# Side work of a scan kernel in smaller pieces, and in another order

## The chip, the cores and the metric

The kernel runs on one core of a Trainium2 chip. The metric is the device time of one execution in microseconds (us). Before the change three executions took 6510.28, 6516.89 and 6527.06 us; the median is 6516.89 us. The profile shown below is of one execution of 6514.5 us.

## The reference

Two layers follow one another. Layer 0 is a selective scan over images, layer 1 a spectral (Fourier) attention layer. The change touches only layer 0, which computes, for 4 images of 48 x 48 places and 128 channels:

```python
xz = einsum('bhwc,ec->bhwe', groupnorm(x), in_proj_w)   # 128 -> 2 x 256 channels
xin, z = split(xz)
xc = silu(depthwise_conv3x3(xin) + conv_b)              # nine taps a channel
xs = [x0, x1, x0 reversed, x1 reversed]                 # row order and column order, each both ways
dts, Bs, Cs = x_proj_w[k] @ xs[k]                       # 8 + 16 + 16 rows
dt = softplus(dt_proj_w[k] @ dts + dt_proj_b)
# for each of 256 channels and 16 states, along 2304 places:
h = h * exp(dt * A) + (dt * u) * B
y = sum over states of h * C
# the four directions are summed, D * xs is added, then layer norm over 256 channels,
# times silu(z), times out_proj_w; the result is added to x
```

Layer 1 takes the result, and its code is the same in both kernels.

## The kernel before

**Tiles and loops.** An image's 2304 places are cut into five chunks of 480 places (the last has 384). The 256 channels are two halves (`f` = 0, 1) of 128 partitions. The outermost loop runs over 16 passes, numbered here from 0: pass 4 b + q is image b (0 to 3) in the q-th direction of `ORDER = (0, 2, 1, 3)`. Directions 0 and 2 go along the rows, forwards and backwards, 1 and 3 along the columns. A pass has 5 chunks, a chunk has 16 steps, one for each state, so there are 1280 steps.

**A step** is spread over the engines by `advance`, which calls ten small stages with different lags, so that ten steps are under way at a time. In a step TensorE spreads one row of B over 128 partitions (`spread`, tile `pb`, skipped in one step of four); VectorE multiplies it by dt * u (`drive_in`, tile `db`); ScalarE computes the two halves of exp(dt * A) (`decay`, tile `da`, in PSUM) and copies the carry of the last chunk; VectorE runs the recurrence along the chunk (`scan`, tile `h`); GpSimd multiplies by C (`read_out`, tile `hc`); TensorE adds the two halves to the sums over states by multiplying with the identity (`sum_up`, tile `yp`). In the one step of four that has no `pb`, GpSimd makes `db`.

**Side work.** Everything else of layer 0 is written as Python generators that wait in the queue `later`, and is interleaved with the steps. A call of `piece()` takes the next generator and lets it emit instructions up to its next `yield`. `advance` calls `piece()` once at the end of every step. A bare `yield` keeps the generator as the current one, so that the next piece is also its own. `yield FREE` lets the next piece start again at the head of the queue, and `yield WAIT` passes the turn on at once. What is emitted in a piece stands in each engine's queue right behind the step's own instructions, because `Ordered` keeps all instructions of an engine in the order in which they are written. Side tiles in PSUM all use the one bank with tag `pp` (`side`) after the start.

These are the generators:

- `boot` prepares image 0: for each chunk the input projection (`project_in`, tiles `pj` and `pad`), the convolution (`convolve`, tiles `pc` and `xc`, nine matmuls with diagonal matrices `cdiag`, one a tap), and the chunk's projections (`project_chunk`: `px`, two matmuls; two small corrections with `less`; `pd`, two matmuls). In pass 0 a second `piece()` follows every step.
- `front(b)` does the same for a whole further image b, apart from the chunk projections. Each half first has nine `taps` and a memset of `pad` on GpSimd, then five input projections, then five convolutions. It ends with a Silu over all of `xc`.
- `project` does the chunk projections of the next pass, and waits (`WAIT`) when it is a ring of seven chunks ahead.
- `back` ends a chunk of an image: after its last direction, layer norm (tiles `pm`, `pv`), the gate (`pz`), the output projection (`po`, `pr`) and the store. Its work tile `ws` has the same single buffer (tag `pad`) that `front` uses for `pad`, and both use the single buffer of `x`. So the next image's `front` can't be started before the last `back` has ended.

**Order of the side work before.** `upcoming` appends the next pass's `project` at the end of `later`. At the start of chunk 2 of an image's first pass, all remaining `back`s are drained, that is, their pieces are emitted one after the other without steps between, and then `front(b + 1)` is appended. At the start of the image's last pass, `drain(coming)` emits what is left of `front`. `drain(nxt)`, close to the end of each pass, does the same for the next pass's `project`.

**Pieces before.** `convolve` yields after every third tap, and goes on with the next chunk's first taps in the piece in which it emits the copy of the previous one; `front` yields `FREE` only around whole halves. `project_chunk` has both `px` matmuls in one piece. `back` yields twice after `pm`, after `po` and after `pr`.

Of the kernel before, what the change touches and what calls it, by code (L numbers as in the profile page):

```python
# [19 lines left out]
B, T, H, W = 4, 48, 48, 128  # L20
# [33 lines left out]
def layer0(ctx, tc, io, x1_dram):  # L54
# [107 lines left out]
    def like(ap, k):  # L162

        return ap if k % 2 == 0 else ap.rearrange("p (w h) -> p w h", h=T)
# [32 lines left out]
    def project_in(b, f, x, made, pad, s, n):  # L197

        r0, nr = s // H, n // H
        pj = side(f"pj{b}_{f}_{s}")  # L200
        on.tensor.matmul(
            pj[:, 0:n], made["w"][:, f * 128 : (f + 1) * 128], x[:, 0, s : s + n], start=True, stop=True
        )
        yield
        on.scalar.activation(
            pad[:, 1 + r0 : 1 + r0 + nr, 1 : 1 + H],
            pj[:, 0:n].rearrange("p (r c) -> p r c", c=H),
            AF.Identity,
            bias=made["wb"][:, f : f + 1],
        )  # L210

    def convolve(b, f, cdiag, pad, xc, s, n):
        r0, nr = s // H, n // H
        pc = side(f"pc{b}_{f}_{s}")
        for j in range(9):
            dy, dx = divmod(j, 3)
            on.tensor.matmul(
                pc[:, 0:n].rearrange("p (r c) -> p r c", c=H),
                cdiag[:, j],
                pad[:, r0 + dy : r0 + dy + nr, dx : dx + H],  # L220
                start=(j == 0),
                stop=(j == 8),
            )
            if j % 3 == 2:
                yield
        on.scalar.activation(xc[:, f, s : s + n], pc[:, 0:n], AF.Identity, bias=cb[:, f : f + 1])

# [29 lines left out]
    def front(b, made):  # L257


        x = load_x(b, "x")  # L260
        yield FREE
        yield from open_up(b, x, made)
        xc = made["xc"]
        for f in range(NF):
            cdiag = one.tile([128, 9, 128], F32, tag="cdiag", name=f"cdiag{b}_{f}")
            taps(cdiag, f)
            pad = one.tile([128, T + 2, H + 2], F32, tag="pad", name=f"pad{b}_{f}")
            on.gpsimd.memset(pad, 0.0)
            yield FREE
            for s, n in CHUNKS:  # L270
                yield from project_in(b, f, x, made, pad, s, n)
            for s, n in CHUNKS:
                yield from convolve(b, f, cdiag, pad, xc, s, n)
            yield FREE
        for f in range(NF):
            on.scalar.activation(xc[:, f], xc[:, f], AF.Silu)
        yield
# [6 lines left out]
    def project_chunk(c, w_dt, xc):  # L284


        k, s, n = c.k, c.s, c.n
        src = at(xc, k, s, n)
        px = side(f"px{c.t}")
        for f in range(NF):  # L290
            on.tensor.matmul(
                like(px[0:NX, 0:n], k), w_xp[:, k, f], src[:, f], start=(f == 0), stop=(f == NF - 1)
            )
        yield
        xd = two.tile([32 + R, LC], F32, tag="xd", name=f"xd{c.t}")
        on.scalar.copy(xd[:, 0:n], px[0 : 32 + R, 0:n])
        c.cd = dram.tile([2 * N, LC], F32, tag="cd", name=f"cd{c.t}")
        nc.sync.dma_start(c.cd[:, 0:n], xd[0 : 2 * N, 0:n])

        c.bs = ring.tile([NX, LC], BF16, tag="bs", name=f"bs{c.t}")  # L300
        on.scalar.copy(c.bs[:, 0:n], px[0:NX, 0:n])
        for q in range(2):
            on.tensor.matmul(px[0:NX, 0:n], less[:, q], c.bs[:, 0:n], start=False, stop=True, skip_group_check=True)
            yield
            rows = slice(64 + 32 * q, NX)
            on.scalar.copy(c.bs[rows, 0:n], px[rows, 0:n])
        c.dt = ring.tile([128, NF, LC], F32, tag="dt", name=f"dt{c.t}")
        for f in range(NF):
            pd = side(f"pd{c.t}_{f}")
            on.tensor.matmul(  # L310
                pd[:, 0:n],
                w_dt[32 : 32 + R, f * 128 : (f + 1) * 128],
                xd[32 : 32 + R, 0:n],
                start=True,
                stop=True,
            )
            yield
            on.scalar.activation(c.dt[:, f, 0:n], pd[:, 0:n], AF.Identity, bias=b_dt[:, k, f : f + 1])
# [22 lines left out]
    def back(b, s, n, yb, x, w, wb):  # L341


        t = f"{b}_{s}"
        xs = at(x, 1, s, n)[:, 0]
        ys = yb[:, :, 0:n]
        ws = one.tile([128, (T + 2) * (H + 2)], F32, tag="pad", name=f"ws{t}")
        z = ws[:, 0 : NF * LC].rearrange("p (f n) -> p f n", f=NF)
        rs, xo = ws[:, NF * LC : (NF + 1) * LC], ws[:, (NF + 1) * LC : (NF + 2) * LC]
        pm = side(f"pm{t}")  # L350
        for f in range(NF):
            on.tensor.matmul(pm[:, 0:n], lnmat, yb[:, f, 0:n], start=(f == 0), stop=(f == NF - 1))
        yield
        yield
        on.vector.tensor_sub(ys, ys, pm[:, None, 0:n].to_broadcast([128, NF, n]))
        yield
        on.scalar.activation(z[:, :, 0:n], ys, AF.Square)
        pv = side(f"pv{t}")
        for f in range(NF):
            on.tensor.matmul(pv[:, 0:n], lnmat, z[:, f, 0:n], start=(f == 0), stop=(f == NF - 1))  # L360
        yield
        on.scalar.activation(rs[:, 0:n], pv[:, 0:n], AF.Sqrt, bias=eps)
        for f in range(NF):
            pz = side(f"pz{t}_{f}")
            on.tensor.matmul(
                like(pz[:, 0:n], 1), w[:, D + f * 128 : D + (f + 1) * 128], xs, start=True, stop=True
            )
            yield
            if f == 0:
                on.vector.reciprocal(rs[:, 0:n], rs[:, 0:n])  # L370
            on.scalar.activation(z[:, f, 0:n], pz[:, 0:n], AF.Identity, bias=wb[:, NF + f : NF + f + 1])
        on.scalar.activation(z[:, :, 0:n], z[:, :, 0:n], AF.Silu)
        yield
        on.gpsimd.tensor_mul(ys, ys, z[:, :, 0:n])
        yield
        po = side(f"po{t}")
        for f in range(NF):
            on.tensor.matmul(po[:, 0:n], w_out[:, 0, f], yb[:, f, 0:n], start=(f == 0), stop=(f == NF - 1))
        yield
        yield  # L380
        on.vector.tensor_mul(xo[:, 0:n], po[:, 0:n], rs[:, 0:n])
        pr = side(f"pr{t}")
        on.tensor.matmul(like(pr[:, 0:n], 1), ident, xs, start=True, stop=False)
        for f in range(NF):
            on.tensor.matmul(pr[:, 0:n], w_out[:, 1, f], z[:, f, 0:n], start=False, stop=(f == NF - 1))
        yield
        yield
        on.vector.tensor_add(xo[:, 0:n], xo[:, 0:n], pr[:, 0:n])
        nc.sync.dma_start(x1_dram[b].rearrange("w h t -> w (h t)")[:, s : s + n], xo[:, 0:n])
        yield FREE  # L390
# [129 lines left out]
    ORDER = (0, 2, 1, 3)  # L520
# [18 lines left out]
    def drain(gen):  # L539
        while gen in later:  # L540
            piece()
# [27 lines left out]
    def upcoming(j):  # L569

        c = directions[j][0]
        gen = project(c.b, c.k, directions[j], c.im["xc"])
        later.append(gen)
        return gen

    first = directions[0]
# [5 lines left out]
        drive(first[0], f)  # L582
    for j, chunks in enumerate(directions):
        b, k = chunks[0].b, chunks[0].k
        if k == ORDER[-1]:
            if b + 1 < B:
                drain(coming)
            images[b]["x"] = load_x(b, "xr")
        nxt = upcoming(j + 1) if j + 1 < len(directions) else None
        on.gpsimd.memset(carries[j % 2], 0.0)  # L590
        for m, c in enumerate(chunks):
            c.carry = carries[j % 2]
            if k == ORDER[0] and b + 1 < B and m == 2:
                while backs:
                    drain(backs.popleft())
                coming = front(b + 1, images[b + 1])
                later.append(coming)
            for i in range(N):
                if i in (N // 2 + 3, N // 2 + 6):
                    f = int(i > N // 2 + 3)  # L600
                    if m + 1 < len(chunks):
                        while not (j or chunks[m + 1].ready):
                            piece()
                        drive(chunks[m + 1], f)
                    elif nxt is not None:
                        drain(nxt)
                        drive(directions[j + 1][0], f)
                advance(Step(c, i))
                if not j:
                    piece()  # L610
    for _ in range(len(window)):
        advance(None)
# [629 lines left out]
```

## Time and profile before

| | |
|---|---|
| time, median of three | 6516.89 us |
| layer 0, up to the last store's work | about 4428 us of 6514.5 |
| busy: VectorE, TensorE, GpSimd, ScalarE | 5274.4, 4831.0, 4730.3, 3057.8 us |
| mean of one scan, of one `hc` | 2129 ns, 2140 ns |
| mean of one `db` on VectorE | 1108 ns |
| scans, `hc` products | 1280 each |

How to read it: most instructions of layer 0 carry the line L50, because the helper class there emits them, so groups are told apart by their tiles. A group's line gives the busy time, the mean of one instruction, and after the bar the time for which its engine stood idle just ahead of it, with what ended that idle time. A matrix product in 32 bits shows as two records of MATMUL in the trace. A windows line gives a stretch, its length, the busy time of PE, PEld (weight loads), DVE (VectorE), ACT (ScalarE) and POOL (GpSimd) with the number of instructions, the granted TensorE clock as a share of full speed, the share of the DMA engines and GB/s.

### The profile page before, as it was taken

How to read it: one execution, taken by the hardware profiler on the slowest of the kernel's cores; microseconds unless marked ns; L12 is line 12 of the kernel's file. 1: busy time of each engine (PE TensorE's matmuls, PEld its weight loads, DVE VectorE, ACT ScalarE, POOL GpSimd, SP SyncE). 2: the span in 40 equal slices, each digit the busy share in tenths (PEclk: the TensorE clock that was granted, in tenths of full speed). 3: DMA queues.
4: the chain of work that ended last, by engine and by line, in shares of the span. 5: the costliest groups of instructions: out<-in, count | busy, mean ns of one | idle time of the engine just before them, and what ended most of it. 6: DMA issues, size and time to landing. Idle time of an engine off the chain costs nothing. (4 is left out here: it accounts for less than half of the span.)

```text
span 6514.5 us, 45606 instructions
## 1 busy us (share of the span) xinstructions
PE 4831.0 (74%) x12654; PEld 2223.1 (34%) x12654; DVE 5274.4 (81%) x3788; ACT 3057.8 (47%) x6652; POOL 4730.3 (73%) x2641
## 2 busy tenths in 40 slices
PE   6788778889887888977888877784233498878663
PEld 2343333334333333433333333332122244435332
DVE  2559999977999987899999999983799899963444
ACT  3546666655666655656666656552000133312222
POOL 3659998877999878899988999981665499941212
PEclk8999999999999999999999999997566655557776
DMA  1213333222323322233323323322200100020222
GB/s 45 67 61 104 99 94 98 93 86 80 100 100 99 93 90 77 95 99 98 99 91 106 100 99 99 96 81 54 48 1 0 19 5 4 4 43 5 59 59 58
DMA packets 268514, 457.52 MB, mean 70 GB/s; under 512 B 83870, under 2 KB 193470, under 8 KB 268258
## 3 DMA queue, kind: packets, MB, share of 16 engines
q1 hardware_dynamic: 221282, 438.00, 21.9%
q10 hardware_dynamic: 46976, 16.61, 1.4%
q8 instruction: 99, 1.62, 0.1%
q14 instruction: 157, 1.29, 0.1%
HBM read 419.47 MB, written 35.02 MB: 70 GB/s over the span
## 5 line engine op out<-in xcount | busy, mean ns | idle before, releaser
L50 POOL TENSOR_TENSOR hc<-h,cbc 128x960 f32<-128x960 f32 (+1 forms) x1280 | 2721.5, 2140 | 651.7 <-DVE h L50 418.3
L50 DVE TENSOR_TENSOR_SCAN h<-da,carry,db 128x961 f32<-128x961 f32 (+1 forms) x1280 | 2700.9, 2129 | 139.8 <-ACT carry L50 126.2
L50 PE MATMUL yp<-hc,ident 128*128 128x480 f32 (+1 forms) x5120 | 2285.4, 575 | 0.0
L50 ACT ACTIVATE da<-dt,a_neg 128x480 f32<-128x480 f32 (+1 forms) x2560 | 1660.4, 649 | 1260.6 <-DVE h L50 1215.2
L50 PEld LDWEIGHTS yp<-hc,ident 128*128 128x128 f32 x5120 | 1008.6, 199 | 1537.2 <-issue 1102.9
L50 DVE TENSOR_TENSOR db<-du,pb 128x960 f32<-128x960 f32 (+1 forms) x960 | 1063.8, 1108 | 414.6 <-PE pb L50 362.3
L50 PE MATMUL pb<-bs,pick 112*128 112x480 bf16 (+1 forms) x960 | 360.0, 375 | 543.6 <-DVE db L50 541.7
L50 POOL TENSOR_TENSOR db<-du,bbc 128x960 f32<-128x960 f32 (+1 forms) x320 | 687.8, 2149 | 0.0
L1007 PE MATMUL py<-attn_t,xt 48*128 48x384 f32 x768 | 509.8, 849 | 76.3 <-DVE m L1015 71.6
L1009 ACT COPY ysb<-py 128x384 f32<-128x384 f32 x384 | 183.9, 479 | 404.1 <-PE py L1007 360.4
L1007 PEld LDWEIGHTS py<-attn_t,xt 48*128 48x128 f32 x768 | 234.8, 321 | 338.3 <-issue 153.1
L50 PE MATMUL pc<-pad,cdiag 128*128 128x480 f32 (+1 forms) x630 | 270.2, 570 | 17.6 <-ACT pad L50 14.6
L50 ACT COPY db<-carry 128x1 f32<-128x1 f32 x1280 | 226.0, 177 | 22.8 <-DVE db L50 20.4
L50 POOL TENSOR_TENSOR du<-dt,xc 128x480 f32<-128x480 f32 (+1 forms) x160 | 204.7, 1279 | 36.8 <-ACT dt L50 36.8
L927 PE MATMUL pat<-ident,s 48*48 48x48 f32 x128 | 13.3, 277 | 275.3 <-POOL s L923 275.3
L50 PE MATMUL px<-xc,w_xp 128*112 128x480 f32 (+1 forms) x320 | 204.4, 768 | 10.6 <-ACT xc L50 9.6
L50 PE MATMUL yp<-y,ident 128*128 128x480 f32 (+1 forms) x240 | 178.3, 876 | 40.2 <-ACT y L50 40.2
L50 PEld LDWEIGHTS <-pick 112*128 112x128 bf16 x960 | 98.3, 102 | 307.7 <-issue 291.0
L1020 POOL TENSOR_TENSOR zi<-zi,m 128x384 f32<-128x384 f32 x192 | 191.8, 999 | 14.5
L1018 POOL TENSOR_TENSOR zi<-gw,ysb 128x384 f32<-128x384 f32 x192 | 181.6, 946 | 25.4 <-ACT ysb L1009 25.0
L1019 POOL TENSOR_TENSOR m<-gw,ysb 128x384 f32<-128x384 f32 x192 | 186.0, 969 | 9.4 <-ACT ysb L1009 9.4
L50 ACT COPY carry<-h 128x2 f32<-128x2 f32 x1024 | 192.6, 188 | 0.0
(269 smaller groups left out, 5675.7 us busy)
## 6 DMA issues: line engine op xcount, KB each, us to landing
cbc<-cd SPq DMA_DIRECT2D x512, 480.0 KB
bbc<-cd SPq DMA_DIRECT2D x256, 240.0 KB
cbc<-cd SPq DMA_DIRECT2D x128, 384.0 KB
bbc<-cd SPq DMA_DIRECT2D x64, 192.0 KB
da_wM<-a_wM SPq DMA_DIRECT2D x12, 396.0 KB
x<-in_xT SPq DMA_DIRECT2D x16, 288.0 KB
xr<-in_xT SPq DMA_DIRECT2D x16, 288.0 KB
e_wM<-de_wM SPq DMA_DIRECT2D x12, 384.0 KB
```

The source lines that it names most:

```text
L50: return lambda *args, **kw: self._tc.keep_in_program_order(emit(*args, **kw))
L927: nc.tensor.transpose(pt[:, h], s[:, h], ident[0:T, 0:T])
L1007: nc.tensor.matmul(p[:, 0 : HG * T], xt[:, c, j], attn_t[:, b, hs], start=True, stop=True)
L1009: nc.scalar.copy(ysb[:, c], py[c])
L1018: nc.gpsimd.tensor_mul(zi[:, hs], gr, ysb[:, 1])
L1019: nc.gpsimd.tensor_mul(t2, gi, ysb[:, 0])
L1020: nc.gpsimd.tensor_add(zi[:, hs], zi[:, hs], t2)
```

## The change

The change alters no arithmetic. It cuts the side work of layer 0 into pieces of one or two matmuls, lets the generators interleave at more places, and changes their priority. In `convolve` the nine taps are emitted as 2, 2, 2, 2, 1 for images 0 and 1, and as 2, 1, 1, 1, 1, 1, 2 for images 2 and 3; the copy out of PSUM that follows is a piece of its own, since `front` now yields `FREE` after each input projection and each convolution. The two `px` matmuls of a chunk become two pieces. In `back` one of the two yields after `pm` and after `po` is gone, several become `FREE`, and `pr` is split. The next pass's `project` goes to the head of the queue, except that of pass 1, which stands behind `boot`. `front(b + 1)` is no longer preceded by a drain: it is appended from chunk 2 on, as soon as no `back` is left in the queue, so it follows the `project`s and the `back`s. In pass 0 the second piece a step stops once the last chunk is ready. The purpose is that side work shall fit into the gaps of the steps rather than hold them up.

```diff
     def convolve(b, f, cdiag, pad, xc, s, n):
+        ends = (1, 3, 5, 7, 8) if b < 2 else (1, 2, 3, 4, 5, 6, 8)
...
-            if j % 3 == 2:
+            if j in ends:
                 yield
...
             for s, n in CHUNKS:
                 yield from project_in(b, f, x, made, pad, s, n)
+                yield FREE
             for s, n in CHUNKS:
                 yield from convolve(b, f, cdiag, pad, xc, s, n)
-            yield FREE
+                yield FREE
...
                 like(px[0:NX, 0:n], k), w_xp[:, k, f], src[:, f], start=(f == 0), stop=(f == NF - 1)
             )
-        yield
+            yield
...
             on.tensor.matmul(pm[:, 0:n], lnmat, yb[:, f, 0:n], start=(f == 0), stop=(f == NF - 1))
         yield
-        yield
         on.vector.tensor_sub(ys, ys, pm[:, None, 0:n].to_broadcast([128, NF, n]))
-        yield
+        yield FREE
...
         on.scalar.activation(z[:, :, 0:n], z[:, :, 0:n], AF.Silu)
-        yield
+        yield FREE
         on.gpsimd.tensor_mul(ys, ys, z[:, :, 0:n])
-        yield
+        yield FREE
...
         yield
-        yield
         on.vector.tensor_mul(xo[:, 0:n], po[:, 0:n], rs[:, 0:n])
         pr = side(f"pr{t}")
         on.tensor.matmul(like(pr[:, 0:n], 1), ident, xs, start=True, stop=False)
+        yield
         for f in range(NF):
             on.tensor.matmul(pr[:, 0:n], w_out[:, 1, f], z[:, f, 0:n], start=False, stop=(f == NF - 1))
-        yield
         yield
...
-        later.append(gen)
+        if j == 1:
+            later.append(gen)
+        else:
+            later.appendleft(gen)
         return gen
...
+        if k == ORDER[0]:
+            coming = None
...
-            if k == ORDER[0] and b + 1 < B and m == 2:
-                while backs:
-                    drain(backs.popleft())
-                coming = front(b + 1, images[b + 1])
-                later.append(coming)
             for i in range(N):
+                if k == ORDER[0] and b + 1 < B and m > 1 and coming is None and not any(g in later for g in backs):
+                    coming = front(b + 1, images[b + 1])
+                    later.append(coming)
...
                 advance(Step(c, i))
-                if not j:
+                if not chunks[-1].ready and not j:
                     piece()
```

## The prediction

> **What bounds the kernel now.** I read the page's totals first, then its groups, then cut the first layer into its 16 passes (image by direction, 80 scans each, cut at the first scan of each pass) and asked for busy times by pass.
>
> ```profile
> PE 4831.0 (74%) x12654; PEld 2223.1 (34%) x12654; DVE 5274.4 (81%) x3788; ACT 3057.8 (47%) x6652; POOL 4730.3 (73%) x2641
> DVE  2559999977999987899999999983799899963444
> ...
> L50 POOL TENSOR_TENSOR hc<-h,cbc 128x960 f32<-128x960 f32 (+1 forms) x1280 | 2721.5, 2140 | 651.7 <-DVE h L50 418.3
> L50 DVE TENSOR_TENSOR_SCAN h<-da,carry,db 128x961 f32<-128x961 f32 (+1 forms) x1280 | 2700.9, 2129 | 139.8 <-ACT carry L50 126.2
> ...
> L50 DVE TENSOR_TENSOR db<-du,pb 128x960 f32<-128x960 f32 (+1 forms) x960 | 1063.8, 1108 | 414.6 <-PE pb L50 362.3
> ```
>
> VectorE leads; its digits are 9 almost everywhere in the first layer (up to 4428 us) except at the start and in two dents. The third row names what it waits for there: `pb`, one small matmul per step. By pass (windows; columns are length, then busy PE, PEld, DVE, ACT, POOL, then clock):
>
> ```profile
> 85.30:506.90 421.60, 342.55 (x820) 152.16 (x820) 236.81 (x156) 214.94 (x444) 235.83 (x131) 0.91 0.19 61
> 1254.50:1564.90 310.40, 261.34 (x636) 118.11 (x635) 241.46 (x162) 169.33 (x382) 240.85 (x135) 0.92 0.27 85
> 1564.90:1822.80 257.90, 213.35 (x522) 93.65 (x521) 229.26 (x142) 157.52 (x364) 221.75 (x111) 0.95 0.29 95
> 1822.80:2063.20 240.40, 192.36 (x450) 80.58 (x449) 228.00 (x142) 149.15 (x352) 223.61 (x112) 0.95 0.31 99
> 2063.20:2326.20 263.00, 221.63 (x518) 93.51 (x518) 246.75 (x156) 174.69 (x380) 233.03 (x116) 0.95 0.31 95
> 3398.00:3647.40 249.40, 205.05 (x494) 88.87 (x492) 234.42 (x148) 160.89 (x368) 223.36 (x113) 0.94 0.31 101
> ```
>
> These are passes 0, 4, 5, 6, 7 and 12. VectorE's work is nearly the same in all (228 to 247), the length is not: 12 us of VectorE idle in pass 6, 15 in pass 12 (no next image), but 69 in pass 4, 29 in pass 5, 185 in pass 0. The long ones are exactly those in which `front` or `boot` runs. Pass 8 (308.8) and 9 (258.1) repeat 4 and 5. The time order inside a convolution stretch of pass 8, first on PE, then on DVE:
>
> ```profile
> 2560.94 1.77 PE L50 MATMUL yp<-hc,ident 128*128 128x480 f32 x4
> 2562.55 2.10 PE L50 MATMUL pc<-pad,cdiag 128*128 128x384 f32 x6
> 2564.49 0.37 PE L50 MATMUL pb<-bs,pick 112*128 112x480 bf16 x1
> ...
> 2564.90 1.16 DVE L50 TENSOR_TENSOR db<-du,pb 128x960 f32<-128x960 f32 x1 [0.47 <-PE pb L50]
> 2565.97 2.21 DVE L50 TENSOR_TENSOR_SCAN h<-da,carry,db 128x961 f32<-128x961 f32 x1
> 2568.65 1.16 DVE L50 TENSOR_TENSOR db<-du,pb 128x960 f32<-128x960 f32 x1 [0.47 <-PE pb L50]
> ```
>
> One f32 matmul is two records, so `x6` is a piece of three taps. `pb` for the next step is queued behind it: PE sets the step. And the drain of an old `back` in pass 4 (DVE):
>
> ```profile
> 1346.61 3.15 DVE L50 RECIPROCAL ws<-ws 128x480 f32<-128x480 f32 x1 [5.36 <-ACT ws L50]
> 1359.86 0.66 DVE L50 TENSOR_TENSOR ws<-po,ws 128x480 f32<-128x480 f32 x1 [10.09 <-PE po L50]
> 1364.08 0.66 DVE L50 TENSOR_TENSOR ws<-ws,pr 128x480 f32<-128x480 f32 x1 [3.56 <-PE pr L50]
> ```
>
> The scans around it start at 1338.0 and 1365.7: 27.7 us for one step.
>
> [...] `pb` starts only when the six `pc` records are through. [...] I use distances of starts: four `yp` records take 2562.55-2560.94 = 1.61 us, 0.40 each, 0.8 a matmul. [...] the trace's loads are 1.28.
>
> **The price of a step.** VectorE at 480 columns: 2.21 + 3/4 of 1.16 = 3.08, less the small overlap; undisturbed chunks of 16 steps last 48.2, so 3.01. PE: 1.61 for `yp` plus 0.20 for `pb` = 1.8. With a piece of three taps (2.4) it is 4.2, two taps 3.4, one tap 2.6. So three taps cost about 1.2 us a step, one tap nothing, two taps 0.4 if several follow one another, less what an empty piece after them gives back. The program's order shows where the pieces fall after the change: no step outside pass 0 holds more than two full-width side matmuls; for images 2 and 3 the nine taps go 2,1,1,1,1,1,2 and then an empty piece (9 in 8 steps, 2.7 us on average); for image 1 they go 2,2,2,2,1 and empty (9 in 6 steps, 1.8+1.2 = 3.0, even with VectorE).
>
> **Part by part.**
> *Passes 4 and 8.* The drain at `m == 2` goes (19 us of VectorE waits: 10.1 + 5.4 + 3.6). All three-tap pieces go: VectorE's `pb` waits there sum to 38.8. What remains is pass 12's pattern (249.4, the same `back` work) plus `open_up`'s statistics on VectorE (241.5-234.4 = 7 us): 256. That is -54 and -53.
> *Passes 5, 6, 9, 10.* The convolutions move here, one piece a step. At full clock they hide. The clock of 0.95 means half speed for a tenth of the time, 8 steps a pass; there a one-tap step costs 5.2 instead of 3.0, and about half the steps hold a tap: 8 x 1/2 x 2.2 = 9 us at most, of which some is absorbed (pass 6 had only 2.5 us of `pb` waits, though half-speed steps without side work should cost 8 x 0.6 = 5). I take 247 for 5 and 9 (-11 each), 248 and 249 for 6 and 10 (+8 each).
> *Passes 1, 2.* Image 1's front comes here from pass 0, in twos: +8 and +10, bounded by 0 and by 20 (half-speed two-tap steps at 6.8: 4 x 3.8 = 15, and 5 from runs of twos).
> *Pass 0.* Chunk by chunk it takes 106.0, 82.5, 95.9, 95.9, 41.3. `boot` goes from 14 pieces a chunk to 19, 7 to 9.5 steps at two pieces a step. One boot chunk takes 44.7 us now (read-outs at 148.3 and 193.0), of which PE work is 19.6 (24.5 matmuls) + 7 x 1.8 = 32; with 9.5 steps it is 37 and about 48 with the same waits. In the new order three boot chunks remain after the first read-out and end at the last step of chunk 2, 31 steps in: 3 x 48 + 8 = 152 for the first two chunks against 174 now (read-outs at 114.8 and 288.3), and some 6 earlier at the start because less stands ahead: -28. In chunks 3 to 5 two pieces a step of six taps (a step of 6.65: `pc` at 336.91, then 343.56) become one project piece: 49.5 x 2 + 41.3 + 5.5 for the Softplus burst + 3 for `open_up` = 149 against 229: -80. Together -108.
> *Passes with `back` (3, 7, 11, 15).* VectorE fills 246.75 of 263. Three of its operations per `back` now follow their matmul by one step, not two (`pm`, `po`, `pr`). What waits behind them is the next `db` and scan. By the time of the scan ahead of them PE has had about 3 us for 1.6 us of matmuls, so between 0 and a step of 3 us each; I take 0.1 on average: +1 each. Splitting `px` and `pr` works the other way.
> *Hidden.* `taps` and the memset hold POOL for 7.4 us (5.25 + 2.19), as now; POOL has 224 of 240 us in a pass, and four `h` buffers cover two steps. Two more table loads in the whole order: [...] in no term. Passes 12 to 14: -1.
>
> Sum: -108 +8 +10 +1 | -54 -11 +8 +1 | -53 -11 +8 +1 | -1 +1 = -200. 6516.9 - 200 = 6317. The second layer (2086 us) has the same instructions.
>
> **Rivals.**
> *PE fills (6389).* Nothing is absorbed at half speed: passes 1 and 2 +20, 6 and 10 +15, 5 and 9 -2.5, the `back` passes +5. Sum -108+40-107+25+20 = -130, 6387; with two loads 6389. For it: PE busy of 192 to 213 in these passes plus 40 us of taps nears 240. Against it: pass 6 as it is.
> *All hidden (6277).* No loss in 1, 2, 6, 10 (-34), 3 less in 4 and 8: 6277. For it: 48.2 us chunks now carry two-matmul pieces of `px` with no loss.
> *No change (6510).* The time returns as waits of ScalarE: `pad` waits for POOL, scans for ScalarE (126 us now). Against: these waits come with the clusters.
> *Slower (6575).* Each of 60 one-step waits behind `pm`, `po`, `pr` costs a whole step of 3.1: +186 on top of the PE rival. For it: VectorE is the bound of these passes. Against: `reciprocal` already follows ScalarE by one step and idled 16.2 us in 16 of them.
>
> **Chances.** Forecast 0.66, PE fills 0.17, all hidden 0.10, no change 0.03, slower 0.04. Faster 0.93, same 0.03, slower 0.04. Range 6265 to 6400: it holds the first three and reaches a little past the outer two, because pass 0's boot (48 us a chunk) is the least certain term.
>
> **What would show it.** Pass 4 and 8 near 256, pass 0 near 314, passes 5, 6, 9, 10 at 245 to 250; no three-tap or six-tap run of `pc` behind the first read-out but in boot; `db`'s waits for `pb` down from 362 to under 200. It would be wrong if `pb` waits reappear in passes 1, 2, 5, 6, or if `pm`, `po`, `pr` show up as VectorE's releasers.

## The result, and the profile after

The changed kernel takes 6298.86 us (median of four, 6295.47 to 6304.09) against 6519.11 us for the kernel before in the same measurement: a ratio of 0.9663, 95% interval 0.9646 to 0.968. The forecast was 6317 in a range of 6265 to 6400.

The page's totals, and its group of `db`, the operation that had waited for `pb`:

```profile
PE 4767.9 (76%) x12654; PEld 2208.8 (35%) x12654; DVE 5269.7 (84%) x3788; ACT 3059.5 (49%) x6654; POOL 4724.5 (75%) x2641
DVE  3789999989999999999999999963999899954444
...
L50 DVE TENSOR_TENSOR db<-du,pb 128x960 f32<-128x960 f32 (+1 forms) x960 | 1061.9, 1106 | 208.9 <-PE pb L50 152.9
```

VectorE has no less to do: its busy time went from 5274.4 to 5269.7, the mean of one `db` of 960 columns from 1148 to 1146 ns. TensorE's fell by 63 us with the same 12654 records, so its records became shorter, not fewer. The two dents in VectorE's digits are gone. What fell is the idle time ahead of `db`, from 414.6 to 208.9, and in it the waits for `pb`, from 362.3 to 152.9. Both sums hold one long wait ahead of the first scan (54.6 and 50.3 us). Within the 16 passes the waits for `pb` fell from 303.9 to 99.3: 79 of that in pass 0, and 72 in passes 4 and 8. Passes 0, 1, 4, 5, 6 and 7, cut again at the first scan of each (length, busy PE, PEld, DVE, ACT, POOL, clock):

```profile
80.90:397.80 316.90, 258.82 (x632) 115.82 (x630) 234.88 (x156) 197.80 (x421) 225.96 (x120) 0.92 0.24 76
397.80:638.70 240.90, 215.76 (x554) 96.66 (x552) 228.98 (x141) 153.32 (x364) 227.60 (x121) 0.99 0.32 101
...
1153.70:1413.70 260.00, 215.14 (x525) 94.58 (x525) 239.68 (x163) 162.15 (x373) 233.48 (x124) 0.93 0.30 97
1413.70:1655.30 241.60, 214.14 (x541) 95.97 (x541) 228.79 (x141) 149.24 (x357) 228.04 (x122) 0.98 0.33 104
1655.30:1900.50 245.20, 220.29 (x532) 94.60 (x531) 228.42 (x142) 159.95 (x365) 226.04 (x113) 0.97 0.32 99
1900.50:2170.90 270.40, 226.57 (x525) 96.81 (x525) 247.02 (x155) 179.69 (x386) 230.52 (x115) 0.93 0.30 92
```

Passes 1 and 5 now hold about half of an image's convolutions each and are no longer than the 240.4 to 241.6 that passes without any took before. (Passes 13 and 14, which hold none, now take 237.3 and 239.2.) The 16 passes together, the last one counted to the end of the last scan, are 210.0 us shorter, the start before the first scan 4.4, the tail of layer 0 2.7, the second layer 3.8: 220.9 us, by which the two profiled spans differ.

A convolution in pass 5 of the changed kernel in order of time, first PE, then DVE:

```profile
1476.49 1.77 PE L50 MATMUL pc<-pad,cdiag 128*128 128x480 f32 x4
1478.10 0.37 PE L50 MATMUL pb<-bs,pick 112*128 112x480 bf16 x1
1478.31 1.77 PE L50 MATMUL yp<-hc,ident 128*128 128x480 f32 x4
1479.92 0.97 PE L50 MATMUL pc<-pad,cdiag 128*128 128x480 f32 x2
...
1476.86 1.16 DVE L50 TENSOR_TENSOR db<-du,pb 128x960 f32<-128x960 f32 x1
1477.93 2.21 DVE L50 TENSOR_TENSOR_SCAN h<-da,carry,db 128x961 f32<-128x961 f32 x1
1480.25 1.16 DVE L50 TENSOR_TENSOR db<-du,pb 128x960 f32<-128x960 f32 x1
```

A piece is two or four records (one or two taps), `pb` is through at 1478.47 while the scan still runs, and `db` follows without a wait.

### The profile page after: what moved, and what is told of

It is laid out like the page before. It is cut to its first block, busy times and chain, and to the rows that moved or that the text cites. A ratio compares the mean times of both kernels' runs of the same rounds, so it can differ in the third digit from the quotient of the medians.

```text
span 6293.6 us, 45620 instructions
## 1 busy us (share of the span) xinstructions
PE 4767.9 (76%) x12654; PEld 2208.8 (35%) x12654; DVE 5269.7 (84%) x3788; ACT 3059.5 (49%) x6654; POOL 4724.5 (75%) x2641
## 3 DMA queue, kind: packets, MB, share of 16 engines
q14 instruction: 156, 1.28, 0.1%
## 5 line engine op out<-in xcount | busy, mean ns | idle before, releaser
L50 DVE TENSOR_TENSOR db<-du,pb 128x960 f32<-128x960 f32 (+1 forms) x960 | 1061.9, 1106 | 208.9 <-PE pb L50 152.9
L50 PE MATMUL pc<-pad,cdiag 128*128 128x480 f32 (+1 forms) x630 | 283.3, 561 | 10.7 <-ACT pad L50 10.7
L50 PE MATMUL pd<-xd,w_dt 8*128 8x480 f32 (+1 forms) x320 | 168.7, 607 | 39.9 <-ACT bs L50 25.6
```

Source lines behind the costliest of these rows:

```text
L50: return lambda *args, **kw: self._tc.keep_in_program_order(emit(*args, **kw))
```

## The experiments

"Order alone" and "Without the drain alone" start from the kernel before, all others from the changed kernel. Ratios are to the kernel before, measured together with each run. Lengths of passes are from each run's profile, cut in the same way, in us.

**Pieces alone.** The changed kernel with these parts undone:

```diff
-        if j == 1:
-            later.append(gen)
-        else:
-            later.appendleft(gen)
+        later.append(gen)
...
+            if k == ORDER[0] and b + 1 < B and m == 2:
+                while backs:
+                    drain(backs.popleft())
...
-                if not chunks[-1].ready and not j:
+                if not j:
```

> The smaller pieces with the old order: projects at the end of the queue, the drain at chunk 2 and the second piece through all of pass 0 stay. Theory (long runs of taps and the drain each cost VectorE time): passes 5, 6, 9, 10 at 242 to 248, passes 4 and 8 still hold a stall of 20 to 28 us and last about 280, pass 0 is 20 to 40 shorter than 421.6 since a step holds four taps and not six; in all about 6430 us. Rival (only the order matters): no change, 6519. Second rival (only the size of the pieces matters): 6299, as the changed kernel.

6457.53 us, 0.9911 (0.9897 to 0.9926), where about 6430 was expected. Pass 0 is 363.4, 4 and 8 are 270, 6 and 10 are 239. But 5 and 9 grew to 301 and 299, from 258: not foreseen, and taken up again below.

**Order alone.** The kernel before with the new order (projects first, no drain, no second piece in pass 0 once the last chunk is ready) and its old pieces.

> The new order (projects first, no drain, no second piece in pass 0 once the last chunk is ready) with the old pieces of three taps. Theory: passes 4 and 8 lose the stall (20 to 28 us each) but keep their three-tap steps of 4.2 us, 30 steps an image at 1.2 us over VectorE's 3.0; pass 0 gains some 40 to 80 and pass 1 takes up to 40 of it back; in all about 6430 us. Rival (only the order matters): 6299. Second rival (only the size of the pieces matters): 6519.

6444.79 us, 0.989 (0.9875 to 0.9904), again above the 6430 expected. Passes 4 and 8: 284 (from 310); 5 and 9: 268 (from 258); pass 0 357, and pass 1 267.6 instead of 240.8: 65 gained, 27 given back. VectorE's waits for `pb` are still 337.7, from 362.3. Neither half makes more than 75 of the 220 us, and their sum is 135: the rest needs both. In pass 0, the largest single term, the pieces alone give 58, the order alone 65 and both 105. The stop of the second piece in pass 0 was not run by itself, so its own share stays open.

**Without the drain alone.**

```diff
-            if k == ORDER[0] and b + 1 < B and m == 2:
-                while backs:
-                    drain(backs.popleft())
...
+                if k == ORDER[0] and b + 1 < B and m > 1 and coming is None and not any(g in later for g in backs):
```

> The kernel before with one edit: the next image's front is started when no back is left in the queue, not by a drain. Theory: the 27.7 us step of passes 4 and 8 becomes ordinary steps, 20 to 25 us less in each, 6470 us in all. Rival: the backs' work takes its time wherever it stands, and the time stays at 6519. Second rival (the drain is most of the gain): 6400 or less.

6480.55 us, 0.9944 (0.993 to 0.9959). Passes 4 and 8 are 284 (27 and 25 less, about the size of the one stalled step), 5 and 9 are 10 more, which the expectation of 6470 had left out: `front` starts later, so more of it lies in them. The drain was worth 38 us net. Passes 2 to 14 have the same lengths, within 1 us, as with the whole new order. So with pieces of three taps the priority of the projects shortens nothing behind pass 1.

**Three taps again.**

```diff
-        ends = (1, 3, 5, 7, 8) if b < 2 else (1, 2, 3, 4, 5, 6, 8)
+        ends = (2, 5, 8)
```

> The changed kernel with one edit: convolutions yield after every third tap again, with the empty piece after them. Theory: three steps of 4.2 us and one short one, 14.4 us of TensorE work against 12.0 of VectorE, so 2 us a convolution, 10 convolutions a front, 3 images: 60 us more than the changed kernel, 6360, as waits of db for pb in passes 1, 4, 5. Rival (TensorE has room on the average and a buffer of one step is enough): 6299 to 6310.

6371.66 us, 0.9774 (0.9758 to 0.9791): 73 more than the changed kernel, 60 expected. They lie where the convolutions are: pass 1 259.5 (from 240.9), 5 and 9 261 (from 241), 4 and 8 267 (from 260). Within the passes VectorE's waits for `pb` rise from 99.3 to 166.5, which is 67 of the 73 us. Order of time in pass 5 of this run, PE then DVE:

```profile
1477.51 2.58 PE L50 MATMUL pc<-pad,cdiag 128*128 128x480 f32 x6
1479.93 0.33 PE L50 MATMUL pb<-bs,pick 112*128 112x384 bf16 x1
...
1476.42 0.96 DVE L50 TENSOR_TENSOR db<-du,pb 128x768 f32<-128x768 f32 x1 [1.77 <-PE pb L50]
1477.29 1.81 DVE L50 TENSOR_TENSOR_SCAN h<-da,carry,db 128x769 f32<-128x769 f32 x1
1480.29 0.96 DVE L50 TENSOR_TENSOR db<-du,pb 128x768 f32<-128x768 f32 x1 [1.19 <-PE pb L50]
```

The two waits shown, of 1.8 and 1.2 us, stand behind pieces of three taps, here in a chunk of 384 columns. Pass 5 of this run has 20 waits for `pb` of 0.2 to 2.6 us, 19.3 in sum; the changed kernel has 3 there, 1.4 in sum. The empty step after a convolution gives some back, not all. In chunks of 480 columns TensorE's step, from one `yp` to the next with a piece and a `pb` between, has a median of 4.23 us with three taps; in the changed kernel it is 3.43 with two.

**Two taps everywhere.**

```diff
-        ends = (1, 3, 5, 7, 8) if b < 2 else (1, 2, 3, 4, 5, 6, 8)
+        ends = (1, 3, 5, 7, 8)
```

> The changed kernel with the nine taps as 2, 2, 2, 2, 1 for all images. Theory: five steps of 3.4 us and an empty one average 3.0, VectorE's own 3.0, so passes 4 to 6 and 8 to 10 change by no more than 3 us each: 6295 to 6310. Rival (a step over VectorE's 3.0 always costs its excess, 0.4 us in 4 of 6 steps, 20 convolutions): 6330.

6308.81 us, 0.9674 (0.9658 to 0.969), as expected and not the rival's 6330; the interval of the changed kernel overlaps it. Passes 4 and 8 are 263 (+3), 5 and 9 244 (+3), 6 and 10 244 (-1). One or two taps are nearly the same; the step up to three is where it costs.

**No priority for the projects.**

```diff
-        if j == 1:
-            later.append(gen)
-        else:
-            later.appendleft(gen)
+        later.append(gen)
```

> The changed kernel with one edit: every project goes to the end of the queue again. Theory: with small pieces front fills pass 5 and 9 to the end, the project of the next pass is emitted without steps at the pass's end, and VectorE stands for 50 to 60 us in each of passes 5 and 9 (as in the kernel with the pieces alone, where they last 300): 6400 to 6420. Rival (front's FREE yields let project in often enough): 6299 to 6310.

6471.08 us, 0.9926 (0.9912 to 0.9941): of the edits undone one at a time in the changed kernel this one costs most, 172 of the 220 us. The expectation of 6400 to 6420 had the right mechanism for passes 5 and 9 (308 and 310: 67 and 70 more, where 50 to 60 were expected) and had left out pass 1, which does the same (314.8, from 240.9). Pass 5 of this run, PE then DVE:

```profile
1679.87 5.97 PE L50 MATMUL pc<-pad,cdiag 128*128 128x384 f32 x18
...
1746.16 0.58 PE L50 MATMUL pb<-bs,pick 112*128 112x480 bf16 x1
...
1746.78 1.16 DVE L50 TENSOR_TENSOR db<-du,pb 128x960 f32<-128x960 f32 x1 [64.41 <-PE pb L50]
```

One wait of 64 us. Ahead of that `pb` stand the nine taps of a convolution (18 records), and then, in the lines left out, all five chunks of the next pass's `project`: `px`, `less` and `pd` five times over, and not one `yp`. That is `drain(nxt)` at the end of the pass: `front` still stands ahead of the `project` in the queue, so both come out in one step. TensorE was idle for 50.1 of this pass's 308.2 us, for 27.5 of 241.6 in the changed kernel. The same kind of wait, 58 us, lengthened passes 5 and 9 with the pieces alone. With small pieces `front` lasts until there, so what must be ready at the pass's end has to come before it.

**Second yields in `back` again.**

```diff
         yield
+        yield
         on.vector.tensor_sub(ys, ys, pm[:, None, 0:n].to_broadcast([128, NF, n]))
...
         yield
+        yield
         on.vector.tensor_mul(xo[:, 0:n], po[:, 0:n], rs[:, 0:n])
```

> The changed kernel with the second yields after pm and after po put back. Theory: VectorE's waits for pm and po in the passes with backs (3, 4, 7, 8, 11, 15; 6 to 18 us each) go, passes 7 and 15 fall from 270 to 264, in all 30 to 40 us less, 6265. Rival: the time is TensorE's, and comes back as waits of db for pb: within 10 us of 6299. Second rival: two more pieces a back put the front's end into the next pass: slower than 6299.

6297.95 us, 0.9661 (0.9646 to 0.9675): no change in the time, where 6265 was expected. As the first rival had said, the waits came back at `pb`, which rose from 152.9 to 208.1. But they are not spread: 40 of these 55 us lie in passes 4, 8 and 12. The four `back` passes fell (3, 7, 11, 15: 257.7, 258.7, 258.7, 259.8, from 266.0, 270.4, 265.0, 270.5), and passes 4, 8, 12 rose by 11 to 13 each. Pass 7 and 8 of this run, and the longest wait of VectorE in pass 8:

```profile
1905.50:2164.20 258.70, 215.25 (x514) 92.57 (x515) 243.20 (x153) 171.28 (x378) 230.19 (x115) 0.95 0.30 97
2164.20:2435.80 271.60, 223.94 (x532) 97.40 (x532) 243.86 (x165) 168.69 (x377) 233.75 (x125) 0.92 0.29 92
...
2182.17 1.16 DVE L50 TENSOR_TENSOR db<-du,pb 128x960 f32<-128x960 f32 x1 [7.04 <-PE pb L50]
```

VectorE's busy time moved with it (243.20 from 247.02, 243.86 from 239.66): work of a `back` slid into the next pass. The wait of 7.0 us at the start of pass 8 stands behind `px`, `less` and `pd` of the last project chunk, all in one step from 2171.98 to the `pb` at 2181.55; another of 3.3 us follows it, behind the products with `ddiag` and a `pm`. The reading is that the ten extra pieces of a pass had pushed that chunk to the pass's end. The next run puts it to the test.

**The same, with pieces saved elsewhere.** In addition to the edit above, the two `px` matmuls are one piece where the next pass is an image's first:

```diff
-            yield
+            if k or f:
+                yield
```

> The changed kernel with the second yields after pm and po put back, and the pieces for them saved elsewhere: in the project of an image's first direction (which runs in the passes with backs) the two px matmuls are one piece again. Theory: the second yields gained nothing by themselves only because ten more pieces a pass pushed the last project chunk into the emission without steps at the pass's end; without that, VectorE's waits for pm and po (55 us in layer 0) go and at most half comes back as waits for pb: 6260 to 6275. Rival: TensorE's work is the bound in these passes, and the time stays at 6290 to 6300.

6279.67 us, 0.9633 (0.9618 to 0.9647), just above the 6260 to 6275 expected and under the rival's 6290. It is 19 under the changed kernel, with intervals that just overlap. Passes 3, 7, 11, 15 are 259 to 261, and 4, 8, 12 stay at 260, 260, 246, as the reading asked. Pass 0 is 10 longer (327) and the start 4 shorter; `boot` has paired `px` too, but why this lengthens pass 0 was not followed up. VectorE's waits in layer 0 up to 4190 us, first of the changed kernel, then of this run:

```profile
DVE db L50 <- PE pb L50: 152.9, 80, 50.3
...
DVE ws L50 <- PE po L50: 40.1, 17, 3.6
...
DVE yb L50 <- PE pm L50: 14.9, 5, 6.5
```

```profile
DVE db L50 <- PE pb L50: 178.6, 93, 46.5
...
DVE ws L50 <- PE po L50: 10.4, 1, 10.4
DVE yb L50 <- PE pm L50: 7.5, 1, 7.5
```

Of the 55 us behind `po` and `pm`, 48.5 lay in the passes, and all of that is gone: the 18 us of this run are one wait of each, in the tail of the layer. 26 come back at `pb`, or 30 within the passes alone, which is more than the half expected at most.

**Slower boot.**

```diff
-                if not chunks[-1].ready and not j:
+                if not chunks[-1].ready and not j and i % 3:
```

> The changed kernel, but in pass 0 the second piece is left out in every third step while boot runs. Theory: boot is as long as its TensorE work and its waits, and each step under it is one that need not be done later; boot covers four steps more, so pass 0 falls by 3 to 4 steps, 10 us, from 317 to 307. Rival (boot's waits grow with its steps): 317 or more. Second rival (steps with two pieces are so much dearer than their TensorE work that every step without one counts): 295 or less.

6296.43 us, 0.9653 (0.9634 to 0.9673). Pass 0 is 302.6, 14 less (10 expected), and the start 5 less; pass 1 gives 12 back (252.8). No measurable change.

**Two of them together.** Slower boot and second yields, without the saved pieces.

> The changed kernel with the second yields after pm and po and the slower boot together. Theory: the two gains add, 6255. Rival: either gives nothing, 6265 to 6299.

6288.02 us, 0.9646 (0.963 to 0.9662), not the 6255 of two gains that add. That is in the rival's range: passes 4, 8 and 12 are again at 261 to 272, and the interval does not tell it from the changed kernel.

**All three.** Second yields, paired `px`, slower boot.

> The second yields after pm and po, the paired px in the passes with backs, and the second piece of pass 0 left out in every third step, together. Theory: the backs' gain stays (passes 3, 7, 11, 15 at 259 to 261) and boot's share adds a few us at the start: 6265 to 6280, under the changed kernel's 6299 by more than both intervals. Rival: what pass 0 gains pass 1 gives back, as with the slower boot alone, 6280 to 6290.

6272.91 us, 0.9626 (0.9613 to 0.9639), as expected, the fastest here, and the only one whose interval lies wholly under that of the changed kernel. Pass 1 again gives back 12 of what pass 0 gains, and whether the boot's share adds anything to the 6279.67 without it stays open.

**Idle steps filled.** A matmul whose result nobody uses, in each step whose piece found no side work:

```diff
+        if begun[0]:
+            idle = side(f"idle{spare_n[0]}")
+            spare_n[0] += 1
+            on.tensor.matmul(idle[:, 0:LC], ident, w_in[:, 0:LC], start=True, stop=True)
...
+    spare_n = [0]
```

> The changed kernel with one more matmul (480 columns, result not used) in each step whose piece found no side work. Theory: half speed comes when TensorE idles, so the granted clock in passes 12 to 14 rises from 0.94 to 0.98 or more, VectorE's waits for pb don't grow, and the time stays or falls by up to 15 us. Rival (half speed comes from load): the clock falls below 0.94 and the time grows by 10 us or more.

6305.57 us, 0.9676 (0.9661 to 0.9691): no measurable change against the changed kernel. Passes 13 and 14 of this run, which have no other side work than projects:

```profile
3437.90:3675.00 237.10, 215.63 (x547) 96.90 (x547) 228.75 (x141) 146.06 (x352) 222.43 (x112) 0.98 0.32 103
3675.00:3916.70 241.70, 224.69 (x548) 97.58 (x548) 228.12 (x141) 147.06 (x348) 223.60 (x112) 0.99 0.31 98
```

The clock is 0.98 and 0.99; in the changed kernel it is 0.94 in both, at 237.3 and 239.2 us. More matmuls, a higher clock, and the same length within 3 us. The rival, a lower clock and 10 us more, fell.

## Why the prediction was right

**The bound.** VectorE behind `pb`, behind taps, is shown: with three taps a piece 67 us of waits for `pb` return, with two they hardly do (6.1 us in pass 5, against 19.3 with three and 1.4 in the changed kernel). The price of a step held: 4.23 us measured for three taps against 4.2, and 3.43 for two against 3.4.

**Terms of the sum**, predicted and measured: pass 0 -108, -104.7. Passes 4 and 8 -54 and -53, -50.4 and -48.8. Passes 5 and 9 -11 each, -16.3 and -17.7. Passes 1 and 2 +8 and +10, +0.1 and +8.5. Passes 6 and 10 +8 each, +4.8 and +3.3. The `back` passes 3, 7, 11, 15 +1 each, -0.3, +7.4, +1.6, +6.3. All 16: -200, -210.0. Passes 0, 4 and 8 carry 204 of the 210, and there the forecast was right in its mechanism. That the sum of the passes came within 10 us is in part luck, since the errors below have different signs: 29 too slow in six passes, 11 too fast in the `back` passes, 8 too fast in passes 4 and 8.

**The step that was wrong: a cost at half speed.** The forecast charged passes 1, 2, 5, 6, 9 and 10 for taps that run at half speed. Its reading of the clock comes out of the trace. In the kernel before, the granted clock is recorded as 1.0 or as 0.5, with 25 us at 0.5 in pass 2, and there the four records of a `yp` take about twice the 1.77 us of full speed:

```profile
932.79 3.40 PE L50 MATMUL yp<-hc,ident 128*128 128x480 f32 x4
```

The cost was not there. The six passes were forecast at 1491 us together (249, 251, 247, 248, 247, 249) and took 1462.0. They spend 72 us at half speed instead of 154, so the forecast had carried the clock of before over. But that is not what decides it: of their 19.4 us of waits for `pb`, only 0.8 stand within or up to 1.5 us behind a stretch at half speed. (With two taps everywhere some of this cost is there: about 3 us each in passes 6 and 10, which are then 27 us at half speed.) In the filled run, with more matmuls in the steps that had no side work, the granted clock of passes 13 and 14 went from 0.94 to 0.98 and 0.99. A forecast that reckoned with this would have had a better clock, and still the wrong place of the cost.

What passes 2, 6 and 10 did lose lies elsewhere. Pass 2 has 9.0 us of waits for `pb`, from 2.3, which the forecast had named as a sign against it, and its two largest stand at full speed behind a `px` of a column direction (PE, then DVE):

```profile
703.05 1.77 PE L50 MATMUL px<-xc,w_xp 128*112 128x480 f32 x2
704.64 0.38 PE L50 MATMUL pb<-bs,pick 112*128 112x480 bf16 x1
...
705.06 1.16 DVE L50 TENSOR_TENSOR db<-du,pb 128x960 f32<-128x960 f32 x1 [1.99 <-PE pb L50]
```

Two records, one matmul, take 1.59 us there and not the 0.8 of the price; `yp<-y`, two operations earlier, is as slow (two records in 1.61 us, from 699.82 to 701.43). Passes 2, 6 and 10 also hold a wait of 4.0 to 4.8 us for ScalarE, which runs the Silu at the end of `front`; for images 2 and 3 it stood in passes 5 and 9 before, and that move is a part of what 5 and 9 gained beyond the forecast. So pass 2 came near its +10 by luck.

**What was mis-sized the other way: one step between matmul and VectorE.** The prediction took 0.1 us on average for 60 such places. The waits behind `pm`, `po` and `pr` are 52 us in the 16 passes, 0.9 a place. They were partly paid before under another name: in the four `back` passes 36 us of them are new, while the waits for `pb` fell from 47.0 to 19.7, and two of these passes show +7.4 and +6.3. That these releasers appear was named as a sign against the forecast. The sign came, and the net loss was small. With the second yields and room for them, the `back` passes are at 259 to 261: the waits were real time.

**What the prediction did not see.** It credited the drain and the small taps, and gave the projects' priority no term. Its absence costs 172 us. The prediction could leave it out because it read the final order of the program, in which the priority is already there. The gains do not add: pieces alone 61, order alone 74, both 220.

**Smaller readings.** The two more table loads came (6654 instructions of ScalarE, 6652 before). They cost little: in both traces a load takes 1.28 us, and the next instruction of ScalarE starts 1.29 us behind the load's start at the median. And the 16.2 us for which `reciprocal` had idled were three waits of 5.4 us, two in the drains and one in the tail; where it was interleaved with steps it had not waited at all.

**Rivals.** "PE fills" fell: passes 1 and 5, with half of an image's convolutions each, are at 240.9 and 241.6. "All hidden" gave 6277, 22 us from the result where the forecast is 18. It was closer in passes 1 and 10, not in 2, 6, 4 and 8. "Slower" fell, as did "no change": the scan's waits for ScalarE in the 16 passes went from 140 to 121 us in sum.

## What to carry to other kernels

When a bound engine waits for one small instruction on a shared engine that works off what stands ahead of it first, as TensorE did here (in the kernel before, the six `pc` records of 2562.55, then the `pb` at 2564.49), count what stands ahead in each step in starts, not ends (four `yp` records are listed with 1.77 us, and the next operation starts 1.61 us behind their start), and cut side work so that a step's sum stays under the bound engine's step. Cutting work into small pieces stretches it in time, so whatever has a deadline must be moved to the front of the queue in the same edit. Pieces are a budget: adding two to each `back` pushed another generator over its deadline, and a gain showed only when as many were saved elsewhere.

## What was not expected of the hardware

TensorE's granted clock rose with the load placed in its gaps: 0.95 to 0.99 in pass 1 (busy from 185.96 to 215.76 us), and 0.94 to 0.98 by useless matmuls in pass 13 (185.91 to 215.63 us). The share of busy time alone does not set it: in the changed kernel pass 4, busy 215.14 of 260.00 us, has 0.93, and pass 13, busy 185.91 of 237.30 us, 0.94. And the higher clock gained nothing in passes 13 and 14, where VectorE's waits for `pb` had been 0.6 and 3.9 us: they took 237.1 and 241.7 us, against 237.3 and 239.2 in the changed kernel.

A `px` of a column direction took twice the time of one of a row direction at the same clock: in the changed kernel the next operation starts 1.59 us behind its two records of 480 columns (703.05 to 704.64), and 0.80 us behind those of a row direction (1165.95 to 1166.75), both at a granted clock of 1.00.
